# A graph layer on one core: the aggregation's copy and store move to ScalarE, the product weights get a pool of their own, and two products cross a seam between phases

## The chip, the cores and the metric

The kernel runs on one core of a Trainium2 chip. A core has five engines that run side by side, each through its own instructions in order: TensorE (PE, with PEld for its weight loads), VectorE (DVE), ScalarE (ACT), GpSimd (POOL) and SyncE (SP), which here does nothing but issue transfers. ScalarE and GpSimd can issue transfers too. The metric is the device time of one execution in microseconds (us), less is better. Before the change the median of 3 runs is 1910.45 us (1910.1 to 1912.72).

## The reference

One layer over 32 graphs of 512 nodes and 256 features, float32. After a layer norm and a relu, each graph goes through a convolution branch and a message branch, and a gated unit joins them:

```python
h = jnp.maximum(_layernorm(x), 0.0)
# inside the layer, with x for h:
xc = jnp.transpose(x, (0, 2, 1))
c = relu(bn(conv1d(xc, conv1_w, 0)))            # 1 tap
c = bn(conv1d(c, conv2_w, 8))                   # 17 taps
x_conv = jnp.transpose(relu(c + xc), (0, 2, 1))
s = x @ w_se.T + b_se                           # 3 features for each node
A = jnp.exp(-squared_distances(s)) * mask       # mask = adj
msg = relu(x @ w_msg.T + b_msg)
x_nmp = jnp.einsum('bnm,bmd->bnd', A, msg)      # the aggregation
# gi, gh: products of [x_conv, x_nmp] and x with w_ih and w_hh
r, z = sigmoid(gi_r + gh_r), sigmoid(gi_z + gh_z)
n = tanh(gi_n + r * gh_n)
out = x_before_norm + (1 - z) * n + z * x
```

## The kernel before

The 17-tap convolution is done by frequencies: windows of 64 nodes are transformed (`xf`), each frequency unit `u` of 40 is multiplied by the transformed weights (`WD`, in DRAM), and the results (`YD`, in DRAM) are transformed back later. The graphs are cut into two groups of 16. The phases are: first part of group 0 (norm, first convolution, windows to frequencies, and the weights to frequencies), nodes of group 0 (messages, `A`, aggregation, with the 40 products spread between), first part of group 1, nodes of group 1, and then the gated unit for pairs of graphs, from about 911 us to the end. In the first parts the instructions stand in the order in which the program records them; in the nodes phases a scheduler orders them at build time.

The parts that the change and the steps below touch:

```python
    WT, WSUM = {}, {}

    def load_unit(pw, g, u):
        t = WT[g, u] = pw.tile([P, 2, DC, D], FP, tag="wt", name=f"wt_{g}_{u}", bufs=3)
        for k in range(2):
            nc.sync.dma_start(t[:, k], WD[2 * u + k].rearrange("(i p) o -> p i o", p=P))

    def sum_unit(pw, g, u):
        t = WSUM[g, u] = pw.tile([P, DC, D], FP, tag="wsum", name=f"wsum_{g}_{u}", bufs=2)
        nc.gpsimd.tensor_tensor(t, WT[g, u][:, 0], WT[g, u][:, 1], op=ALU.add)

    def product(pw, g, u, xf):
        if (g, u) not in WT:
            load_unit(pw, g, u)
        if u > 0 and (g, u) not in WSUM:
            sum_unit(pw, g, u)
        wt = WT.pop((g, u))
        re, im = xf[:, :, 2 * u, :], xf[:, :, 2 * u + 1, :]
        wr, wi = wt[:, 0], wt[:, 1]
        y = pw.tile([P, 3, D], FP, tag="y", name=f"y_{g}_{u}", bufs=3)
        p = bank(f"py_{g}_{u}")
        if u == 0:
            terms = [(p[:, :D], re, wr), (p[:, D : 2 * D], im, wi)]
        else:
            both = pw.tile([P, 2, DC, P], FP, tag="both", name=f"both_{g}_{u}", bufs=2)
            nc.gpsimd.tensor_tensor(both[:, 0], re, im, op=ALU.add)
            nc.gpsimd.tensor_tensor(both[:, 1], im, re, op=ALU.subtract)
            wsum = WSUM.pop((g, u))
            p2 = bank(f"py2_{g}_{u}")
            terms = [(p2[:, :D], both[:, 1], wr), (p[:, D : 2 * D], both[:, 0], wi), (p[:, :D], re, wsum)]
        for dst, v, w in terms:
            for ic in range(DC):
                nc.tensor.matmul(dst, v[:, ic, :], w[:, ic, :], start=(ic == 0), stop=(ic == DC - 1))
        for k in range(2):
            nc.scalar.copy(by_half(y[:, k, :]), halves(p[:, k * D : (k + 1) * D]))
        if u == 0:
            nc.vector.memset(y[:, 2, :], 0.0)
        else:
            nc.vector.tensor_copy(by_half(y[:, 2, :]), halves(p2[:, :D]))
        nc.scalar.dma_start(YD[g][:, 3 * u : 3 * u + 3, :], y)

```

```python
# VectorE takes mean and variance and normalises, GpSimd takes the power -1/2 (rstd)
    def statistics(b):
        stats = work.tile([P, NC, 6], FP, tag="stats", name=f"stats_{b}")
        mv = work.tile([P, NC, 2], FP, tag="mv", name=f"mv_{b}")
        for c in range(NC):
            nc.vector.bn_stats(stats[:, c, :], X[b][:, c, :])
        for c in range(NC):
            nc.vector.bn_aggr(mv[:, c, :], stats[:, c, :])
        rstd = work.tile([P, NC], FP, tag="rstd", name=f"rstd_{b}")
        STATS[b] = mv, rstd
        nc.vector.tensor_scalar(rstd, mv[:, :, 1], LN_EPS, None, op0=ALU.add)
        nc.gpsimd.tensor_tensor(rstd, rstd, minus_half[:, :NC], op=ALU.pow)

    def normalise(b):
        mv, rstd = STATS.pop(b)
        XN[b] = pools["first"].tile([P, NC, D], FP, tag="xn", name=f"xn_{b}", bufs=2)
        for c in range(NC):
            nc.vector.tensor_scalar(
                by_half(XN[b][:, c, :]), halves(X[b][:, c, :]), mv[:, c, 0:1], rstd[:, c : c + 1],
                op0=ALU.subtract, op1=ALU.mult,
            )
        del X[b]

    def transpose_h(b):
        HT[b] = work.tile([P, DC, N], FP, tag="hT", name=f"hT_{b}")
        for dc in range(DC):
            p = bank(f"phT_{b}_{dc}")
            for c in range(NC):
                nc.tensor.transpose(p[:, c * P : (c + 1) * P], XN[b][:, c, dc * P : (dc + 1) * P], ident)
            nc.vector.tensor_scalar(HT[b][:, dc, :], p, 0.0, None, op0=ALU.max)
        nc.sync.dma_start(HD[b], HT[b])
        del XN[b]

    def by_chunks(b):
        HQ[b] = work.tile([P, DC, N], FP, tag="hq", name=f"hq_{b}", bufs=2)
        for ic in range(DC):
            nc.scalar.copy(chunks(HQ[b][:, ic, :]), by_chunk(HT[b][:, ic, :]))
        del HT[b]
    # (cut) message(b): products hq x wmsg into pm; affinity(b): pd, exponentials e on ScalarE,
    # transposes at<-adj and products A = e * at on VectorE
```

```python
# the aggregation, in the nodes phase

    def aggregate(b):
        NMP[b] = work.tile([P, DC, N], FP, tag="nmp", name=f"nmp_{b}")
        for dc in range(DC):
            p = bank(f"pn_{b}_{dc}")
            for mc in range(NC):
                nc.tensor.matmul(p, MSG[b][:, mc, dc * P : (dc + 1) * P], A[b][:, mc, :],
                                 start=(mc == 0), stop=(mc == NC - 1))
            nc.vector.tensor_copy(NMP[b][:, dc, :], p)
        del MSG[b], A[b]

    def save_nmp(b):
        nc.sync.dma_start(ND[b], NMP.pop(b))
```

```python
    def first_part(g, xf, between):


        b0, b1 = g * GB, (g + 1) * GB
        for b in range(b0, b0 + 3):
            if b not in X:
                load_x(b, nc.gpsimd if g else nc.sync)
        statistics(b0)
        normalise(b0)
        statistics(b0 + 1)
        if g == 0:
            transpose_h(b0)
        normalise(b0 + 1)
        if g > 0:
            transpose_h(b0)
        for b in range(b0, b1):
            if b + 3 < b1:
                load_x(b + 3, nc.gpsimd)
            if b == b0:
                conv1(b)
                if g == 0:
                    for steps in between(0):
                        for step in steps:
                            step()
            if b + 2 < b1:
                statistics(b + 2)
            if b + 1 < b1:
                transpose_h(b + 1)
            if b + 2 < b1:
                normalise(b + 2)
            one, two = between(b - b0) if b > 0 else ([], [])
            if b > b0:
                conv1(b)
            for step in one:
                step()
            if b > b0:
                windows_to_freq(b - 1, xf)
            for step in two:
                step()
        by_chunks(b1 - 1)
        load_h(b0)
        windows_to_freq(b1 - 1, xf)
```

```python
# (cut) the phases; `between` of group 0 spreads the transform of the weights
        # (cut)

            def between(b):
                if b % 2 == 0 and b // 2 + 1 < QI // PI:
                    load_taps(gen, b // 2 + 1)
                if 1 <= b <= len(load_weights):
                    load_weights[b - 1]()
                mine = spread(steps, b, GB - 1) if b < GB - 1 else []
                return mine[:1], mine[1:]

            xf = freq_tile(0)
            with tc.manual_schedule():
                first_part(0, xf, between)


# (cut) in nodes(g, xf, last): units = list(range(UNITS)), UNITS is 40
            for i, b in enumerate(todo):
                mine = spread(units, i, last) if i < last else []
                more = i + 1 < GB
                if more:
                    load_adj(todo[i + 1])
                    factors(todo[i + 1])
                for u in mine[:1]:
                    product(pools["pw"], g, u, xf)
                begin(i + 2)
                if more:
                    affinity(todo[i + 1])
                for u in mine[1:2]:
                    product(pools["pw"], g, u, xf)
                aggregate(b)
                save_nmp(b)
                for u in mine[2:]:
                    product(pools["pw"], g, u, xf)

        with phase("pw"):
            with phase("nodes"):
                nodes(0, xf, GB)
            with phase("first", "sums"):
                combine = combine_weights()

                def between(b):

                    if b == GB - 3:
                        for u in range(3):
                            load_unit(pools["pw"], 1, u)
                    two = [partial(sum_unit, pools["pw"], 1, b - GB + 3)] if b > GB - 3 else []
                    return combine[b - 2] if 1 < b < len(combine) + 2 else [], two

                xf = freq_tile(1)
                with tc.manual_schedule():
                    first_part(1, xf, between)
            with phase("nodes"):
                nodes(1, xf, GB - 3)
    outer.close()
```

A name such as `wt_0` is the weights of unit 0; `py` is a product's bank, `pn` the aggregation's, `pm` the message's, `pd` the distances', `pc` the first convolution's, `px` the windows'. `hq` is a copy of `hT` in another order, made by ScalarE. A matrix product of float32 shows as two records in the trace.

Of the kernel before, what the change touches and what calls it, by code (L numbers as in the profile page):

```python
# [57 lines left out]
def gnn_layer(  # L58
# [33 lines left out]
    outer = ExitStack()  # L92
    work = pools["work"] = outer.enter_context(tc.tile_pool(name="work", bufs=2, reuse_waits="tile"))
    early = outer.enter_context(tc.tile_pool(name="early", bufs=1, reuse_waits="tile"))

    def bank(name):
        return psum.tile([P, N], FP, tag="bank", name=name)
# [223 lines left out]

    WT, WSUM = {}, {}

    def load_unit(pw, g, u):
        t = WT[g, u] = pw.tile([P, 2, DC, D], FP, tag="wt", name=f"wt_{g}_{u}", bufs=3)
        for k in range(2):
            nc.sync.dma_start(t[:, k], WD[2 * u + k].rearrange("(i p) o -> p i o", p=P))

# [3 lines left out]

    def product(pw, g, u, xf):
        if (g, u) not in WT:
            load_unit(pw, g, u)
        if u > 0 and (g, u) not in WSUM:
            sum_unit(pw, g, u)
        wt = WT.pop((g, u))
# [23 lines that stand above are left out]
# [80 lines left out]
# [4 lines that stand above are left out]
            for mc in range(NC):  # L446
                nc.tensor.matmul(p, MSG[b][:, mc, dc * P : (dc + 1) * P], A[b][:, mc, :],  # L447
                                 start=(mc == 0), stop=(mc == NC - 1))
            nc.vector.tensor_copy(NMP[b][:, dc, :], p)
        del MSG[b], A[b]  # L450

    def save_nmp(b):
        nc.sync.dma_start(ND[b], NMP.pop(b))

# [251 lines left out]
        return todo[len(todo) * i // n : len(todo) * (i + 1) // n]  # L708


    def first_part(g, xf, between):


        b0, b1 = g * GB, (g + 1) * GB
# [2 lines left out]
                load_x(b, nc.gpsimd if g else nc.sync)  # L717
        statistics(b0)
        normalise(b0)
        statistics(b0 + 1)  # L720
        if g == 0:
            transpose_h(b0)
        normalise(b0 + 1)
        if g > 0:
            transpose_h(b0)
        for b in range(b0, b1):
            if b + 3 < b1:
                load_x(b + 3, nc.gpsimd)
# [21 lines left out]
        by_chunks(b1 - 1)  # L750
        load_h(b0)
        windows_to_freq(b1 - 1, xf)

    @contextmanager
    def phase(*names, bufs=1):
# [5 lines left out]
    with tc.tile_pool(name="freq", bufs=1) as fpool:  # L761
# [3 lines left out]
        with phase("first", "gen"):  # L765
# [7 lines left out]
            def between(b):  # L773
                if b % 2 == 0 and b // 2 + 1 < QI // PI:
                    load_taps(gen, b // 2 + 1)
                if 1 <= b <= len(load_weights):
                    load_weights[b - 1]()
                mine = spread(steps, b, GB - 1) if b < GB - 1 else []
                return mine[:1], mine[1:]

            xf = freq_tile(0)
            with tc.manual_schedule():
                first_part(0, xf, between)


        def nodes(g, xf, last):


            b1 = (g + 1) * GB
            todo = [b1 - 1] + list(range(g * GB, b1 - 1))  # L790
            units = list(range(UNITS))

            def begin(i):
                if i < GB:
                    if todo[i] not in HQ:
# [28 lines left out]

        with phase("pw"):
            with phase("nodes"):
                nodes(0, xf, GB)
            with phase("first", "sums"):
                combine = combine_weights()

                def between(b):

                    if b == GB - 3:
                        for u in range(3):
                            load_unit(pools["pw"], 1, u)
                    two = [partial(sum_unit, pools["pw"], 1, b - GB + 3)] if b > GB - 3 else []
                    return combine[b - 2] if 1 < b < len(combine) + 2 else [], two

                xf = freq_tile(1)
                with tc.manual_schedule():  # L840
                    first_part(1, xf, between)
            with phase("nodes"):
                nodes(1, xf, GB - 3)
    outer.close()


# [92 lines left out]
```

## Time and profile before

| | before |
|---|---|
| time, median of 3 | 1910.45 us |
| span of the profiled execution | 1907.5 us |
| mean granted TensorE clock | 0.988 |
| VectorE copy `nmp<-pn`, 128x512 (L449) | 64 times, mean 674 ns |
| ScalarE copy `p<-pg`, 128x512 (L583) | 32 times, mean 585 ns |
| GpSimd `wsum<-wt` (L331) | 78 times, mean 1413 ns |
| GpSimd `both<-xf` (L347, L348) | 78 times each, mean 752 and 735 ns |
| DMA `wt<-wd` (SyncE) | 160 of 256 KB, 4.5 us to landing (median) |
| DMA `nd<-nmp` (SyncE) | 32 of 512 KB, 3.2 us to landing (median) |

The profile is one execution. For a group of instructions it gives the busy time, the mean of one, and the idle time of the engine just before them with what ended it, as in `[2.52 <-DVE xn L276]`: the engine was idle for 2.52 us until VectorE's write of `xn` released it. In the timeline the columns are the start (us), the duration (us), the engine, line and operation, what it writes and reads, and how many records are joined in the row. `SPq` and `ACTq` are the issues of transfers on SyncE's and ScalarE's queues. The slices cut the span into 40 equal parts, with the busy share in tenths, and `PEclk` is the TensorE clock that was granted, in tenths.

### The profile page before, as it was taken

The numbers are of one execution on the slowest core, as the hardware profiler recorded it, in microseconds if no ns is written. First come the engines' busy times: TensorE is split into PE (matmuls) and PEld (weight loads), VectorE is DVE, ScalarE is ACT, GpSimd is POOL, SyncE is SP. The second block draws the span as 40 slices with busy tenths as digits, with TensorE's granted clock in tenths as the row PEclk, the third lists the DMA queues.
The fourth block names the chain that finished last, engine by engine and source line by source line (L and its number), as shares of the span: only waits on it lengthen the run. The fifth ranks groups of instructions, "written<-read, shape, count | busy, mean of one in ns | idle before, by whom it ended". The sixth has DMA issues, their size and how long they took to land.

```text
span 1907.5 us, 20922 instructions
## 1 busy us (share of the span) xinstructions
PE 1851.2 (97%) x6976; PEld 1114.8 (58%) x6976; DVE 1127.5 (59%) x2234; ACT 563.8 (30%) x1083; POOL 575.7 (30%) x558
## 2 busy tenths in 40 slices
PE   7998999999799899999999999999999999999997
PEld 5776666666698566666555554555455554555443
DVE  7775556564886455555266456645665456655666
ACT  2455434332245333333222221222122221222121
POOL 3330343333332344444413322133212322133210
PEclk9999999999899999999999999999999999999999
DMA  7999888966467788878622554245522554245512
GB/s 207 295 266 228 248 235 248 270 193 202 156 233 198 212 255 265 257 214 239 191 64 67 130 130 109 48 103 130 128 69 62 130 130 98 64 98 130 130 24 43
DMA packets 336954, 309.89 MB, mean 162 GB/s; under 512 B 148567, under 2 KB 286711, under 8 KB 336463
## 3 DMA queue, kind: packets, MB, share of 16 engines
q1 hardware_dynamic: 314783, 248.87, 49.7%
q0 software_dynamic: 7680, 27.30, 5.3%
q10 hardware_dynamic: 14384, 32.39, 4.8%
q8 instruction: 56, 0.92, 0.2%
q14 instruction: 51, 0.42, 0.1%
HBM read 201.60 MB, written 106.89 MB: 162 GB/s over the span
## 4 chain that ended last, share of the span: by engine, by line
PE 64%; DVE 2%; issue 0%; ACT 0%; DVEq 0%
PE pg L556 29%; PE pn L556 15%; PE pc L545 6%; PE pn L447 5%; PE py L354 5%; PE pm L398 2%; PE pd L433 1%; PE psr L422 0%; DVE rz L887 0%; ACT rz L571 0%; DVE rz L687 0%; DVE rz L664 0%; DVE o L694 0%; DVE nt L688 0%; DVE nt L628 0%
## 5 line engine op out<-in xcount | busy, mean ns | idle before, releaser
L534 POOL TENSOR_TENSOR hp<-hp 128x512 f32<-128x512 f32 x64 | 94.7, 1489 | 466.7 <-DMA hp<-hd 423.9
L556 PE MATMUL pg<-hp,sw 128*128 128x512 f32 x448 | 229.9, 595 | 3.1 <-DVE u L588 3.1
L556 PE MATMUL pg<-np,sw 128*128 128x512 f32 x448 | 229.5, 594 | 0.0
L556 PE MATMUL pg<-cp,sw 128*128 128x512 f32 x448 | 228.8, 592 | 0.0
L447 PE MATMUL pn<-A,msg 128*128 128x512 f32 x512 | 225.0, 593 | 0.0
L447 PEld LDWEIGHTS pn<-A,msg 128*128 128x128 f32 x512 | 97.1, 190 | 110.6 <-issue 108.6
L347 POOL TENSOR_TENSOR both<-xf 128x256 f32<-128x256 f32 x78 | 58.7, 752 | 330.4 <-PE py L354 298.6
L354 PE MATMUL py<-wt,both 128*128 128x256 f32 x624 | 151.9, 387 | 6.3 <-DVE at L438 5.6
L571 ACT ACTIVATE rz<-rz,brz 128x512 f32<-128x512 f32 x96 | 69.3, 722 | 276.9 <-DVE rz L575 276.9
L556 PEld LDWEIGHTS pg<-hp,sw 128*128 128x128 f32 x448 | 85.1, 191 | 110.3 <-issue 101.4
L556 PEld LDWEIGHTS pg<-np,sw 128*128 128x128 f32 x448 | 85.4, 191 | 107.7 <-issue 107.7
L556 PEld LDWEIGHTS pg<-cp,sw 128*128 128x128 f32 x448 | 85.3, 190 | 107.5 <-issue 107.5
L354 PEld LDWEIGHTS py<-wt,both 128*128 128x128 f32 x624 | 115.3, 192 | 50.9 <-issue 35.3
L534 POOL TENSOR_TENSOR cp<-cp 128x512 f32<-128x512 f32 x64 | 80.3, 1266 | 186.4 <-ACT cp L550 185.1
L439 DVE TENSOR_TENSOR A<-e,at 128x512 f32<-128x512 f32 x128 | 114.5, 934 | 30.0 <-ACT e L436 29.9
L300 PE MATMUL pc<-w,hT 128*128 128x256 f32 x512 | 124.2, 399 | 4.7 <-DVE hT L288 4.7
L331 POOL TENSOR_TENSOR wsum<-wt 128x512 f32<-128x512 f32 x78 | 110.1, 1413 | 55.7 <-DMA wt<-wd 55.0
L545 PEld LDWEIGHTS pc<-back,yt 120*128 120x128 f32 x1024 | 116.9, 192 | 7.7 <-issue 7.7
L398 PE MATMUL pm<-wmsg,hq 128*128 128x259 f32 x512 | 117.3, 381 | 0.0
L545 PE MATMUL pc<-back,yt 120*128 120x80 f32 (+1 forms) x1024 | 116.2, 274 | 0.0
L633 ACT ACTIVATE nt<-nt,vech 128x512 f32<-128x512 f32 x64 | 46.2, 722 | 233.9 <-DVE nt L632 233.9
L556 PE MATMUL pn<-hp,sw 128*128 128x512 f32 x224 | 115.1, 595 | 0.0
(123 smaller groups left out, 2854.5 us busy)
## 6 DMA issues: line engine op xcount, KB each, us to landing
wt<-wd SPq DMA_DIRECT2D x160, 256.0 KB, 4.5
adj<-in_adj_dram SPq DMA_DIRECT2D x128, 256.0 KB, 5.5
yd<-y ACTq DMA_DIRECT2D x80, 384.0 KB, 5.2
yt<-yd SPq DMA_DIRECT2D x60, 480.0 KB, 7.9
wd<-wst SPq DMA_DIRECT2D x64, 320.0 KB, 5.0
hd<-hT SPq DMA_DIRECT2D x32, 512.0 KB, 4.3
nd<-nmp SPq DMA_DIRECT2D x32, 512.0 KB, 3.2
xb<-in_x_dram SPq DMA_DIRECT2D x128, 128.0 KB, 3.4
```

The costliest lines, as they stand in the source:

```text
L300: nc.tensor.matmul(p[:, j, :], HT[b][:, ic, c * P : (c + 1) * P], w1[:, ic, :], start=(ic == 0), stop=(ic == DC - 1))
L331: nc.gpsimd.tensor_tensor(t, WT[g, u][:, 0], WT[g, u][:, 1], op=ALU.add)
L347: nc.gpsimd.tensor_tensor(both[:, 0], re, im, op=ALU.add)
L354: nc.tensor.matmul(dst, v[:, ic, :], w[:, ic, :], start=(ic == 0), stop=(ic == DC - 1))
L398: nc.tensor.matmul(p[:, : D + NS], hq[:, ic, c * P : (c + 1) * P], wmsg[:, ic, :], start=(ic == 0), stop=(ic == DC - 1))
L439: nc.vector.tensor_mul(A[b][:, mc, :], e, at)
L447: nc.tensor.matmul(p, MSG[b][:, mc, dc * P : (dc + 1) * P], A[b][:, mc, :], start=(mc == 0), stop=(mc == NC - 1))
L534: nc.gpsimd.tensor_tensor(t[:, dst, :], t[:, a, :], t[:, b, :], op=sub)
L545: nc.tensor.matmul(bk[:, t0:t1], YT[p][j * W + w][:, oc * P : (oc + 1) * P], back[:, u0 : u0 + t1 - t0], start=(w == 0), stop=(w == W - 1) ...
L556: nc.tensor.matmul(bk, sw[:, k, q, o, :], terms[k][q], start=(first and i == 0), stop=(i == len(ks) - 1), skip_group_check=True)
L571: nc.scalar.activation(rz[:, g, j, :], src, AF.Sigmoid, bias=brz[:, g : g + 1], scale=1.0)
L633: nc.scalar.activation(n, n, AF.Tanh, bias=b_in[:, i : i + 1], scale=1.0)
```

## The change

The copy of the aggregation out of its bank goes from VectorE to ScalarE, and its store from SyncE's queue to ScalarE's, so that SyncE's loads no longer stand behind a store that waits for the aggregation. The product weights `wt` get a pool of their own that is open through all phases, so that the first three units of group 0 can be loaded at the end of its first part. The last two products of group 0 are recorded inside the first part of group 1, after the first graph's normalisation, to give TensorE work while that graph is normalised; in the same place the first graph's transpose is now ahead of the second graph's normalisation in both groups.

```diff
--- before.py
+++ after.py
@@ -92,6 +92,7 @@
     outer = ExitStack()
     work = pools["work"] = outer.enter_context(tc.tile_pool(name="work", bufs=2, reuse_waits="tile"))
     early = outer.enter_context(tc.tile_pool(name="early", bufs=1, reuse_waits="tile"))
+    wts = outer.enter_context(tc.tile_pool(name="wts", bufs=3, reuse_waits="tile"))
 
     def bank(name):
         return psum.tile([P, N], FP, tag="bank", name=name)
@@ -321,8 +322,8 @@
 
     WT, WSUM = {}, {}
 
-    def load_unit(pw, g, u):
-        t = WT[g, u] = pw.tile([P, 2, DC, D], FP, tag="wt", name=f"wt_{g}_{u}", bufs=3)
+    def load_unit(g, u):
+        t = WT[g, u] = wts.tile([P, 2, DC, D], FP, tag="wt", name=f"wt_{g}_{u}")
         for k in range(2):
             nc.sync.dma_start(t[:, k], WD[2 * u + k].rearrange("(i p) o -> p i o", p=P))
 
@@ -332,7 +333,7 @@
 
     def product(pw, g, u, xf):
         if (g, u) not in WT:
-            load_unit(pw, g, u)
+            load_unit(g, u)
         if u > 0 and (g, u) not in WSUM:
             sum_unit(pw, g, u)
         wt = WT.pop((g, u))
@@ -446,11 +447,11 @@
             for mc in range(NC):
                 nc.tensor.matmul(p, MSG[b][:, mc, dc * P : (dc + 1) * P], A[b][:, mc, :],
                                  start=(mc == 0), stop=(mc == NC - 1))
-            nc.vector.tensor_copy(NMP[b][:, dc, :], p)
+            nc.scalar.copy(NMP[b][:, dc, :], p)
         del MSG[b], A[b]
 
     def save_nmp(b):
-        nc.sync.dma_start(ND[b], NMP.pop(b))
+        nc.scalar.dma_start(ND[b], NMP.pop(b))
 
 
 
@@ -708,7 +709,7 @@
         return todo[len(todo) * i // n : len(todo) * (i + 1) // n]
 
 
-    def first_part(g, xf, between):
+    def first_part(g, freq, between, left=()):
 
 
         b0, b1 = g * GB, (g + 1) * GB
@@ -717,12 +718,12 @@
                 load_x(b, nc.gpsimd if g else nc.sync)
         statistics(b0)
         normalise(b0)
+        for step in left:
+            step()
+        xf = freq(g)
         statistics(b0 + 1)
-        if g == 0:
-            transpose_h(b0)
+        transpose_h(b0)
         normalise(b0 + 1)
-        if g > 0:
-            transpose_h(b0)
         for b in range(b0, b1):
             if b + 3 < b1:
                 load_x(b + 3, nc.gpsimd)
@@ -750,6 +751,7 @@
         by_chunks(b1 - 1)
         load_h(b0)
         windows_to_freq(b1 - 1, xf)
+        return xf
 
     @contextmanager
     def phase(*names, bufs=1):
@@ -775,21 +777,19 @@
                     load_taps(gen, b // 2 + 1)
                 if 1 <= b <= len(load_weights):
                     load_weights[b - 1]()
-                mine = spread(steps, b, GB - 1) if b < GB - 1 else []
+
+                mine = spread(steps, b, GB - 1) if b < GB - 1 else [partial(load_unit, 0, u) for u in range(3)]
                 return mine[:1], mine[1:]
 
-            xf = freq_tile(0)
             with tc.manual_schedule():
-                first_part(0, xf, between)
-
-
-        def nodes(g, xf, last):
+                xf = first_part(0, freq_tile, between)
+
+
+        def nodes(g, xf, units, last):
 
 
             b1 = (g + 1) * GB
             todo = [b1 - 1] + list(range(g * GB, b1 - 1))
-            units = list(range(UNITS))
-
             def begin(i):
                 if i < GB:
                     if todo[i] not in HQ:
@@ -824,7 +824,7 @@
 
         with phase("pw"):
             with phase("nodes"):
-                nodes(0, xf, GB)
+                nodes(0, xf, range(UNITS - 2), GB)
             with phase("first", "sums"):
                 combine = combine_weights()
 
@@ -832,15 +832,15 @@
 
                     if b == GB - 3:
                         for u in range(3):
-                            load_unit(pools["pw"], 1, u)
+                            load_unit(1, u)
                     two = [partial(sum_unit, pools["pw"], 1, b - GB + 3)] if b > GB - 3 else []
                     return combine[b - 2] if 1 < b < len(combine) + 2 else [], two
 
-                xf = freq_tile(1)
+                left = [partial(product, pools["pw"], 0, u, xf) for u in range(UNITS - 2, UNITS)]
                 with tc.manual_schedule():
-                    first_part(1, xf, between)
+                    xf = first_part(1, freq_tile, between, left)
             with phase("nodes"):
-                nodes(1, xf, GB - 3)
+                nodes(1, xf, range(UNITS), GB - 3)
     outer.close()
 
 

```

## The prediction

> **What bounds the kernel now.** I read first the engines' busy time and the slices of the span, then TensorE's own waits, then the timeline around each wait, and last the waits of SyncE's DMA queue. The busy rows and the slices:
>
> ```profile
> PE 1851.2 (97%) x6976; PEld 1114.8 (58%) x6976; DVE 1127.5 (59%) x2234; ACT 563.8 (30%) x1083; POOL 575.7 (30%) x558
> ...
> PE   7998999999799899999999999999999999999997
> ...
> PEclk9999999999899999999999999999999999999999
> ```
>
> TensorE is busy for 1851.2 of 1907.5 us, so all that a change of schedule can win is the other 56.3 us, plus what its matmuls lose at a lowered clock. The change adds and removes no matmul. The slices have three dips: the start, the slice near 480 us and the end. The change touches neither the first 160 us nor the last part. The list of TensorE's waits (total us, times, longest) names the rest:
>
> ```profile
> PE phT L287 <- DVE xn L276: 11.4, 4, 3.5
> PE py L354 <- DVE at L438: 5.6, 1, 5.6
> PE py L354 <- DMA wt<-wd: 5.4, 1, 5.4
> PE pc L300 <- DVE hT L288: 4.7, 2, 3.6
> ```
>
> Three stretches hold what the change can reach, all at seams between phases; the windows from 200 to 400 us and from 640 to 850 us show TensorE 100% busy.
>
> Seam 1, first part 0 into nodes 0: the first product waits for its weights.
>
> ```profile
> 180.44 2.28 SPq L327 DMA_DIRECT2D wt<-wd  x2
> ...
> 188.81 3.48 PE L354 MATMUL py<-wt,xf 128*128 128x256 f32 x8 [5.43 <-DMA wt<-wd]
> 190.87 1.14 ACT L384 COPY hq<-hT 128x512 f32<-128x512 f32 x2 [5.29 <-DMA hT<-hd]
> ```
>
> The last stores of `wd` are issued from 161.41 to 169.76 us, the next graph's `hT` at 169.85 (landed by 177.09), 2 MB of `adj` from 171.30, and `wt_0` only then. In the 5 us windows from 165 to 200 us the DMA share is 0.89 to 1.25: this seam is a queue of bytes.
>
> Seam 2, nodes 0 into first part 1:
>
> ```profile
> 476.32 0.69 DVE L449 COPY nmp<-pn 128x512 f32<-128x512 f32 x1 [2.74 <-PE pn L447]
> 477.85 1.34 DVE L264 BATCH_NORM_STATS2 stats<-x 128x6 f32<-128x256 f32 x4
> 481.39 2.21 PE L287 MATMUL phT<-ident,xn 128*128 128x128 f32 x8 [2.52 <-DVE xn L276]
> 487.24 6.18 PE L300 MATMUL pc<-w,hT 128*128 128x256 f32 x16 [3.64 <-DVE hT L288]
> 497.72 1.93 PE L287 MATMUL phT<-ident,xn 128*128 128x128 f32 x8 [3.43 <-DVE xn L276]
> ```
>
> VectorE is held at the copy of the last aggregation until 476.32 and only then starts the new group's statistics. Idle time is 2.52 + 3.64 + 3.43 = 9.6 us; and the 16 records of `pc` take 6.18 us here against 3.62 at full clock (granted clock 0.60 in 480 to 490).
>
> Seam 3, early in nodes 1:
>
> ```profile
> 633.45 0.34 SPq L453 DMA_DIRECT2D nd<-nmp  x1
> 634.37 2.16 SPq L327 DMA_DIRECT2D wt<-wd  x2
> 639.48 3.43 PE L354 MATMUL py<-wt,both 128*128 128x256 f32 x8 [5.60 <-DVE at L438]
> ```
>
> The wait is put down to a transpose of `adj`, but what lands just then is the weight load issued at 634.37. That load stood in SyncE's queue behind the store of `nmp`. SyncE's queue had issued `adj` until 619.04 and then nothing for 14 us. The queue's own waits say the same for the whole run:
>
> ```profile
> SPq L453 <- DVE nmp L449: 173.0, 30, 16.9
> ```
>
> [...] 8 `py` records after the 5.43 and 5.60 us gaps take 3.48 and 3.43 us against 1.89 elsewhere, so such a gap costs 1.5 to 1.6 us on top of itself. [...] the trace has 585 (`p<-pg`) and 674 ns (`nmp<-pn`).
>
> **The change part by part.**
>
> *Copies and stores to ScalarE.* 64 copies of 0.674 us (43.0 us) leave VectorE, 64 of about 0.585 us (37.4 us) and 32 issues of 0.34 us go to ScalarE. ScalarE is 30% busy, VectorE 59%. In the steady part TensorE never waits, so this alone is worth nothing there. In the built order ScalarE's two copies come right behind the aggregation and ahead of `sl` and `sr`; these are wanted only after a product (2.6 us) and mostly a message block (3.7 us), so no new wait.
>
> *Seam 3.* With the store gone from SyncE, the order there is `adj`, `wt_3`, `hT_18`. The fourth piece of `adj` and `wt_3` (its buffer is free once the first product has run, 615.8) can go out at about 619.5 and land by about 625; `py_3` is wanted at about 633.9. The gap of 5.60 us and the slow 1.54 us (3.43 - 1.89) go: **-7.1 us**.
>
> *Seam 1.* `wt_0` to `wt_2` are now issued at the end of first part 0, but in SyncE's order they come before `hT_0` and `adj`, and the first of them waits for all outstanding stores of `wd`. In the old order bytes moved at about 0.22 MB/us (2.56 MB `wd` from 161.4, then 0.5 MB `hT`, 2 MB `adj`, 0.5 MB `wt_0`, landed at 188.7: 5.6 MB in about 25 us, with 2 us left for the landing). I estimate the wait for `wd` to end near 172.5, 1.5 MB of weights to be through by about 179, `hT_0` landed at 181 to 184 instead of 177.0. Then the message block of graph 0 starts at about 182.5 instead of 177.90: a gap of about 4 us after the `psr` transposes end at 178.1, with the slow clock behind it (1.5). From 182.5: 3.7 + 1.5 for the block, 1.1 `pd`, 0.9 transposes, 1.9 for `py_0` without a wait, 191.6. The old order had `py_0` done at 192.1 and the next block at 192.13, held by `hT_1` (190.87 + its copy). `hT_1` now comes behind 1 MB more of weights and the bubble, 192 to 194. So the gap moves from weights to `hT` and the later point shifts by 0 to +2: **+1 us**, uncertain by 3 either way.
>
> *Seam 2.* Two products (2.6 us each) move behind the last aggregation, and the statistics no longer stand behind its copy. Were that all, the 7.8 us of three products would cover 1.91 (statistics) + 1.04 (`rstd` on GpSimd) + 1.38 (normalise). But the built order on GpSimd is: x loads, `rstd` of graph 16, then `wsum_38`, `both_38`, `wsum_39`, `both_39`. So product 38 waits for `rstd`, which waits for the statistics, which stand on VectorE behind the copy for product 37, which follows the last aggregation. Counting from the end of the last aggregation: that copy starts at 1.06 and ends 1.48; statistics until 3.4; `rstd` 4.45; `wsum_38` 1.27, 5.7; `both_38` 0.72 + 0.73, 7.2. Product 37 ends at 2.6. So TensorE is idle for about 4.7 us before product 38, which then runs 1.5 slower: 11.4; product 39 to 14.0; then `phT` to 15.0 without a wait. The order of transpose and normalise is turned, so `hT` is evicted at once: the `hT` wait shrinks from 3.64 to about 1, `pc_16` ends near 20. The next wait, `phT` of graph 18 (statistics 1.9, `rstd` 1.1, normalise behind the `hT` evictions), stays at about 3.4: `pc_17` starts at about 26. Old order on the same work: the last aggregation would have ended at 476.12 - 5.2 = 470.9, `pc_17` started at 499.44, 28.5. **-2.5 us**.
>
> Sum: -7.1 + 1 - 2.5 = -8.6; 1910.45 - 8.6 = 1901.9, rounded to 1902.
>
> **The rivals.** (a) Seam 2 is hidden as meant, because `rstd` is done before product 38 wants its operands. For it: GpSimd is only 30% busy. Against it: the order in the built program, in which the statistics can't start before product 37. It would take another 6.2 us off (4.7 + 1.5), 1896. (b) Seam 1 gets worse: the wait for `wd` drains the queue, and `hT_0`, `adj` and `hT_1` all come later by the full 1.5 MB. For it: DMA shares near or over 1 there; against it: part of the weights' bytes only trade places. 1.5 MB at 0.22 MB/us is 6.8 us, 6 more than I took: 1908. (c) ScalarE, in order, holds up the exponentials or the sigmoid inputs of the next graph behind its wait for the aggregation, and TensorE waits once in each graph. For it: at the first graph of nodes 1 two exponentials now stand between the two copies. Against it: they are wanted a whole graph later. At 0.5 us in 32 graphs it would more than cancel the gain: 1918. (d) Seam 3 goes on waiting, since `adj` is the true releaser: no gain there, 1909.
>
> **Range and chances.** Seam 3 is the surest (worth 7.1 with a fault of 1.5), seams 1 and 2 by 3 each; root of the squares about 4.5, so 1902 with 1896 to 1909 for 8 in 10. 2% is 38 us: to gain that, two thirds of all idle time in the run would have to go; to lose it, something in every graph would have to wait over 1 us. So 0.02 faster, 0.97 within, 0.01 slower.
>
> **What would show it.** In the changed profile: no wait of `py` for weights of 5 us in nodes 1; a wait of `pm` for `hT` (ScalarE `hq`) near 178 to 182 in place of the 5.43; a wait of `py` for GpSimd `both` or `wsum` of about 5 us near 475; the wait of `pc` for `hT` under 1.5 us; 100% busy windows between 200 and 400 us as before. Wrong if `phT` follows the products with no idle before product 38, if the steady windows fall under 99%, or if the first seam's lost time differs from the old one by over 4 us.

## The result and the profile after

The changed kernel takes 1907.73 us (median of 4 runs, 1904.07 to 1909.81) against 1910.28 (4 runs, 1908.69 to 1912.72) beside it: a ratio of 0.9983 with an interval of 0.9964 to 1.0003. Run once more with later experiments it took 1905.74 us (22 runs) against 1909.84 (43 runs), 0.9979 (0.997 to 0.9988). The first interval includes no gain at all, the second does not. So the change gains 2.6 to 4.1 us. The prediction had 8.45 (1902 against 1910.45).

The busy rows and the slices on the page of the changed kernel (its profiled execution took 1904.07 us, the lowest of the first four):

```profile
PE 1848.2 (97%) x6976; PEld 1112.1 (58%) x6976; DVE 1097.1 (58%) x2170; ACT 598.5 (31%) x1147; POOL 578.7 (30%) x558
...
PE   7998999999899999999999999999999999999997
```

The 64 copies and 32 issues have moved: VectorE has 64 instructions fewer, ScalarE 64 more. The slice from 618 us on, where seam 3 lies, is full now; the one near 480 us is still short, and so is the one from 143 to 190 us, in which seam 1 begins (it was so before). TensorE's waits in the changed kernel (us in total, times, longest):

```profile
PE pm L399 <- ACT hq L385: 9.8, 2, 6.4
PE phT L288 <- DVE xn L277: 8.8, 3, 3.5
...
PE py L355 <- POOL both L349: 4.5, 1, 4.5
...
PE pc L301 <- DVE hT L289: 1.5, 2, 1.1
```

Both waits of `py` for weights are gone. In their place the message block waits twice for `hq` (9.8 us in all), and one product waits for GpSimd.

**Seam 1**, SyncE's queue and TensorE in the kernel before, beside the lines that the prediction shows:

```profile
169.85 1.08 SPq L372 DMA_DIRECT2D hT<-hd  x1
171.30 9.04 SPq L368 DMA_DIRECT2D adj<-in_adj_dram  x8
172.64 3.67 PE L398 MATMUL pm<-wmsg,hq 128*128 128x259 f32 x16
182.84 0.42 SPq L372 DMA_DIRECT2D hT<-hd  x1
199.49 7.03 PE L447 MATMUL pn<-A,msg 128*128 128x512 f32 x16
```

and SyncE's queue, ScalarE and TensorE in the changed kernel:

```profile
160.65 8.32 SPq L250 DMA_DIRECT2D wd<-wst  x8
171.89 3.66 PE L399 MATMUL pm<-wmsg,hq 128*128 128x259 f32 x16
172.75 2.94 SPq L328 DMA_DIRECT2D wt<-wd  x6
175.74 0.47 SPq L373 DMA_DIRECT2D hT<-hd  x1
176.31 10.25 SPq L369 DMA_DIRECT2D adj<-in_adj_dram  x8
...
182.99 1.14 ACT L385 COPY hq<-hT 128x512 f32<-128x512 f32 x2 [5.01 <-DMA hT<-hd]
183.66 5.31 PE L399 MATMUL pm<-wmsg,hq 128*128 128x259 f32 x16 [6.35 <-ACT hq L385]
186.66 1.24 SPq L373 DMA_DIRECT2D hT<-hd  x1
...
195.22 1.14 ACT L385 COPY hq<-hT 128x512 f32<-128x512 f32 x2 [0.58 <-DMA hT<-hd]
195.89 5.53 PE L399 MATMUL pm<-wmsg,hq 128*128 128x259 f32 x16 [3.42 <-ACT hq L385]
...
205.11 7.03 PE L448 MATMUL pn<-A,msg 128*128 128x512 f32 x16
```

SyncE issues nothing for 3.8 us after the last store of `wd` (168.97 to 172.75; the DMA share from 170 to 175 us falls to 0.46, before it was 0.89), then the six weight loads, and only then `hT_0`. The first gap of 6.35 us is followed by a message block at 5.31 us instead of 3.67, the second of 3.42 us by one at 5.53. Gaps and slow blocks lose 6.35 + 1.64 + 3.42 + 1.86 = 13.3 us; before, the 5.43 us wait and the slow product (3.48 - 1.89) lost 7.0. From the first message block of the phase to its first aggregation it took 26.85 us before and takes 33.22 now: **+6.4**.

**Seam 2**, TensorE's timeline in the changed kernel:

```profile
483.78 3.66 PE L355 MATMUL py<-wt,both 128*128 128x256 f32 x8 [4.46 <-POOL both L349]
...
492.21 3.89 PE L301 MATMUL pc<-w,hT 128*128 128x256 f32 x16 [0.45 <-DVE hT L289]
...
500.41 2.27 PE L288 MATMUL phT<-ident,xn 128*128 128x128 f32 x8 [3.43 <-DVE xn L277]
```

The transposes `phT` of the first graph follow the products without a wait, but product 38 waits 4.46 us for GpSimd and then runs slow (3.66 us instead of 1.89, with a granted clock of 0.50 from 484 to 486 us). The `hT` wait is down from 3.64 to 0.45, the last `phT` wait is what it was. **-2.6 us** on the same work, from the fourth message block of nodes 0 to the second convolution block.

**Seam 3**, SyncE's queue and TensorE in the changed kernel:

```profile
605.40 17.14 SPq L369 DMA_DIRECT2D adj<-in_adj_dram  x12
622.65 6.75 SPq L328 DMA_DIRECT2D wt<-wd  x2
...
635.59 1.89 PE L355 MATMUL py<-wt,both 128*128 128x256 f32 x8
```

In the kernel before, the queue's last row ahead of its hole was

```profile
603.51 15.53 SPq L368 DMA_DIRECT2D adj<-in_adj_dram  x11
```

The hole of 14 us (619.04 to 633.45) is filled: the weights go out from 622.65 instead of 634.37, and the product starts without a wait. **-7.3 us** from the first message block of nodes 1 to the fourth. The windows between the seams (220 to 460 and 645 to 900 us) are full as before (TensorE busy for 240.0 of 240 us and 253.9 of 255, before 240.0 and 254.3).

### The profile page after: what moved, and what is told of

Its sections match the earlier page's. It is cut to its first block, busy times and chain, and to the rows that moved or that the text cites. A ratio compares the mean times of both kernels' runs of the same rounds, so it can differ in the third digit from the quotient of the medians.

```text
span 1902.3 us, 20941 instructions
## 1 busy us (share of the span) xinstructions
PE 1848.2 (97%) x6976; PEld 1112.1 (58%) x6976; DVE 1097.1 (58%) x2170; ACT 598.5 (31%) x1147; POOL 578.7 (30%) x558
## 4 chain that ended last, share of the span: by engine, by line
PE 90%; DVE 3%; DMA 3%; SPq 1%; issue 1%; POOL 1%; ACT 0%; POOLq 0%; DVEq 0%; ACTq 0%
PE pg L557 29%; PE pn L557 15%; PE pn L448 11%; PE py L355 11%; PE pc L546 6%; PE pm L399 6%; PE pc L301 4%; PE px L316 3%; PE pw L237 2%; PE pd L434 2%; PE phT L288 1%; DMA ws<-w 1%; PE psr L423 1%; DMA wt<-wd 1%; DVE stats L265 1%
## 5 line engine op out<-in xcount | busy, mean ns | idle before, releaser
L440 DVE TENSOR_TENSOR A<-e,at 128x512 f32<-128x512 f32 x128 | 114.8, 936 | 37.0 <-ACT e L437 36.9
L361 DVE COPY y<-py 128x256 f32<-128x256 f32 x78 | 32.8, 420 | 158.1 <-PE py L355 157.3
L301 PE MATMUL pc<-w,hT 128*128 128x256 f32 x512 | 119.8, 388 | 1.5 <-DVE hT L289 1.5
```

What stands on the lines that cost most here:

```text
L301: nc.tensor.matmul(p[:, j, :], HT[b][:, ic, c * P : (c + 1) * P], w1[:, ic, :], start=(ic == 0), stop=(ic == DC - 1))
L440: nc.vector.tensor_mul(A[b][:, mc, :], e, at)
```

## The experiments

All times are medians, and all ratios are to the kernel before, run beside each batch (1910.28 us in the first, then 1910.63, 1909.84 and 1909.82). For comparison each trace is read in three stages. A goes from the first message block of nodes 0 to the fourth, B from there to the second convolution block of the first part of group 1, and C from the first message block of nodes 1 to the fourth. Each stage holds the same work in all kernels, so that the left-over products need no correction. A, B and C are one trace each.

| kernel | us | ratio (interval) | A | B | C |
|---|---|---|---|---|---|
| before | 1910.28 | | 36.85 | 289.95 | 40.28 |
| changed | 1907.73 | 0.9983 (0.9964 to 1.0003) | 43.23 | 287.35 | 32.97 |
| changed, again | 1905.74 | 0.9979 (0.997 to 0.9988) | 44.65 | 287.99 | 32.97 |
| no early weights | 1899.98 | 0.995 (0.9937 to 0.9963) | 35.20 | 288.10 | 33.00 |
| store on SyncE | 1911.04 | 1.0008 (0.9997 to 1.002) | 41.37 | 288.23 | 40.11 |
| sums first | 1903.65 | 0.9966 (0.9954 to 0.9977) | 41.63 | 284.90 | 32.96 |
| no products left over | 1903.49 | 0.9966 (0.9956 to 0.9976) | 44.16 | 287.16 | 32.97 |
| `hT` first | 1900.74 | 0.9952 (0.9937 to 0.9966) | 36.06 | 288.13 | 32.97 |
| one unit early | 1903.75 | 0.9964 (0.9951 to 0.9978) | 37.42 | 287.09 | 32.96 |
| before + order | 1908.26 | 0.9991 (0.9984 to 0.9998) | 36.11 | 287.38 | 40.15 |
| copy on VectorE | 1903.38 | 0.9963 (0.9949 to 0.9976) | 44.01 | 287.38 | 33.01 |
| before + store | 1901.8 | 0.9954 (0.9941 to 0.9967) | 36.83 | 289.97 | 33.00 |
| two mends | 1895.68 | 0.9925 (0.9912 to 0.9937) | 36.33 | 283.39 | 32.99 |
| two mends, early statistics | 1892.61 | 0.9906 (0.989 to 0.9922) | 34.50 | 281.96 | 32.97 |

Outside these stages one execution differs from the next: the first message block of nodes 0 starts between 170.0 and 176.5 us in these traces, in the changed kernel itself at 171.89 and at 176.54, and the stretch between B and C takes 101.8 to 106.3 us, in the changed kernel itself 102.75 and 106.25. In A kernels with the same loads differ by up to 3.3 us, in B kernels with the same seam by up to 1.1, in C by 0.2. So a stage shows more than the total does, a difference in A from two single traces is uncertain by some 3 us, and differences of totals under 2 us are not read here.

### Leaving out the early weight loads

```diff
-  mine = spread(steps, b, GB - 1) if b < GB - 1 else [partial(load_unit, 0, u) for u in range(3)]
+  mine = spread(steps, b, GB - 1) if b < GB - 1 else []
```

> The changed kernel without the loads of wt_0 to wt_2 at the end of first part 0 (they are left to the nodes phase; in the built order hT_0 stands first again, then wt_0, hT_1, adj). Theory: the first seam lost its time because 1.5 MB of weights go ahead of hT_0 and hT_1 in SyncE's order. From the start of the first message block to the start of the first aggregation the kernel before takes 26.9 us and the changed one 33.2; here it should be 27 or less, and the whole about 6 us less than the changed kernel, 1901 to 1902. Rival: the seam is a queue of bytes and the order does not matter; then 33 us stays and the time stays near 1907. A second rival, that ScalarE's new copies hold up the first seam, also leaves 33 us.

1899.98 us, 5.8 under the changed kernel's 1905.74 of another batch; stage A is down from 43.23 to 35.20. SyncE's queue and TensorE in this kernel:

```profile
166.92 1.19 SPq L373 DMA_DIRECT2D hT<-hd  x1
171.13 0.89 SPq L328 DMA_DIRECT2D wt<-wd  x2
172.12 0.42 SPq L373 DMA_DIRECT2D hT<-hd  x1
172.59 10.32 SPq L369 DMA_DIRECT2D adj<-in_adj_dram  x8
...
175.29 3.67 PE L399 MATMUL pm<-wmsg,hq 128*128 128x259 f32 x16
181.69 1.34 PE L434 MATMUL pd<-sr,sl 9*128 9x512 f32 x8 [2.73 <-ACT sr L425]
184.08 2.81 PE L355 MATMUL py<-wt,xf 128*128 128x256 f32 x8
186.72 3.67 PE L399 MATMUL pm<-wmsg,hq 128*128 128x259 f32 x16
```

Both message blocks run without a wait and at full clock (3.67 us each), and `py_0` does not wait for its weights either, though they were not loaded early. What is left there is a wait of 2.73 us for ScalarE's `sr`, which stands in ScalarE's order behind `hq` of the next graph (179.33), and behind it a lowered clock (0.50 from 183 to 185 us; `py_0` 2.81 instead of 1.89). The early loads cost 8.0 us in this stage by these two traces, and 7.2 by the means of all traces with the three units (43.2, six traces) and without any (36.0, six). ScalarE's copies and the weights' own pool are in this kernel too, so neither is the cause. The loads move bytes that nobody wants yet ahead of bytes that hold up TensorE.

The order here is not that of the kernel before either: there `wt_0` and `hT_1` go out behind eight pieces of `adj` (180.44 and 182.84), here ahead of them (171.13 and 172.12). Stage A is 36.1 to 36.9 us with the old order and 34.5 to 36.3 with this one, three traces each, which do not tell the two apart.

### Putting the store back on SyncE

```diff
-        nc.scalar.dma_start(ND[b], NMP.pop(b))
+        nc.sync.dma_start(ND[b], NMP.pop(b))
```

> The changed kernel with the store of nmp back on SyncE's queue; the copy stays on ScalarE. Theory: in nodes 1 the weights of unit 3 again stand behind the store, TensorE waits 5 to 6 us for them and runs slow for 1.5 us: from the first message block of group 1 to that of its third graph 40 us as before (40.3), not 33.0; whole time about 7 us over the changed kernel, 1914 to 1915. Rival: what mattered was the copy on ScalarE or the own pool of the weights, and the store's queue is nothing: 33 us and 1907.

1911.04 us: stage C is back at 40.11. TensorE's timeline in this kernel:

```profile
639.92 3.63 PE L355 MATMUL py<-wt,both 128*128 128x256 f32 x8 [5.22 <-DMA wt<-wd]
```

The same gap with the same slow product behind it as before (there 5.60 and 3.43 us), and this time the profile names the weights as the releaser. Seam 3 is the place of the store in SyncE's order and nothing else. Without this part, what is left of the change gains nothing that these runs resolve.

### The sums of the left products ahead of the statistics

A function takes the `wsum` and `both` of products 38 and 39 out of `product`, and the first part of group 1 begins with it:

```diff
+        for step in ahead:      # wsum and both of units 38 and 39
+            step()
         statistics(b0)
         normalise(b0)
```

> The changed kernel with GpSimd's sums for products 38 and 39 recorded ahead of the statistics of the first graph, so that they stand before rstd in its order. Theory: the 4.5 us wait of product 38 and its slow matmuls go, and nothing else takes their place, since rstd then ends about 6.4 us after the last aggregation and the transposes are wanted at 7.8: from the end of the last aggregation to the second conv block of group 1 about 20 us instead of 25.9; whole time 6 us less, 1901 to 1902. Rival: the later rstd only moves the wait to the transposes (25 us stays).

1903.65 us; stage B goes from 287.35 to 284.90. TensorE's timeline in this kernel:

```profile
481.13 1.99 PE L364 MATMUL py<-wt,both 128*128 128x256 f32 x8 [1.06 <-POOL both L345]
...
486.69 5.57 PE L301 MATMUL pc<-w,hT 128*128 128x256 f32 x16 [1.82 <-DVE hT L289]
```

The 4.46 us wait shrinks to 1.06, and its slow clock goes (product 38 takes 1.99 us instead of 3.66). That would be 5.1 us (3.4 and 1.7). But only 2.5 come out, because the wait of `pc` for `hT` grows from 0.45 to 1.82 and `pc` now runs at a lowered clock (0.50 from 488 to 490 us). The order on GpSimd was the cause of product 38's wait, and its removal uncovers the next wait on VectorE.

### No products left over

```diff
-                nodes(0, xf, range(UNITS - 2), GB)
+                nodes(0, xf, range(UNITS), GB)
-                left = [partial(product, pools["pw"], 0, u, xf) for u in range(UNITS - 2, UNITS)]
+                left = [partial(product, pools["pw"], 0, u, xf) for u in ()]
```

> The changed kernel with all 40 products of group 0 in its nodes phase, none in the next first part. Theory: the two moved products are worth little, because their sums wait for rstd; without them the statistics come behind the copy of product 39, the transposes wait 2 to 3 us and the hT eviction still comes early, so the second seam costs about what it costs in the changed kernel: whole time within 2 us of it (1905 to 1910). Rival: the moved products are what gained 2.6 us at this seam; without them it falls back to 28.5 us, 1910, or more, because the statistics now wait with nothing beside them (5 us, 1913).

Stage B is 287.16 with all 40 products in the nodes phase, and 287.35 in the changed kernel. TensorE's timeline of this kernel at the seam:

```profile
487.67 2.21 PE L288 MATMUL phT<-ident,xn 128*128 128x128 f32 x8 [2.53 <-DVE xn L277]
490.94 5.60 PE L301 MATMUL pc<-w,hT 128*128 128x256 f32 x16 [1.06 <-DVE hT L289]
```

The wait of `phT` that the two products were to fill is back (2.53), and the wait for GpSimd is gone: the stage is as long. The gain of seam 2 was already there without the products. The time of 1903.49 us (14 runs) lies 7.1 under the kernel before, though the three stages account for 2.8 of it only. In its trace another 2.1 us lie between B and C and 1.0 ahead of A, both of which differ by as much between two executions of one kernel, and its A (44.16) is at the upper end of what these loads gave. Against the changed kernel (1905.74) its interval overlaps. Whether leaving the two products over costs something elsewhere stays open.

### The changed kernel again

> The changed kernel itself, once more beside the kernels of this batch. If the four experiments before it are read rightly, it lies about 7 us above the kernel without the early weight loads (1900.0) and about 7 us under the kernel with the store on SyncE (1911.0): 1904 to 1907. The times of the one run so far go from 1904 to 1910.

1905.74 us over 22 runs, from 1900.32 to 1914.57. Its profiled execution was the slowest of them, 1914.57 us, and is useful for that: compared with the first trace, the start is 4.65 us longer, stage A 1.4, stage B 0.6, C equal, and the stretch between B and C 3.5 (106.25 against 102.75). The profile of one execution can thus lie several us away from the median.

### The order of two lines alone, in the kernel before

```diff
-        if g == 0:
-            transpose_h(b0)
+        transpose_h(b0)
         normalise(b0 + 1)
-        if g > 0:
-            transpose_h(b0)
```

> The kernel before with one line's move alone: the first graph's transpose ahead of the second graph's normalisation in both groups; no products left over, copy on VectorE, store on SyncE, no early weights. Theory: all of seam 2's gain comes from this order: the wait of pc for hT goes from 3.64 to about 1.1, the first part of group 1 starts its second convolution block 2.6 to 2.8 us sooner, time 1908. Rival (the gain comes from the products that fill the gap, or from the copy's leaving VectorE): the time given back at the wait of phT, 1910.6 as before.

1908.26 us, and stage B 287.38 against 289.95: **-2.6**, the whole gain of seam 2. TensorE's timeline:

```profile
478.38 1.89 PE L287 MATMUL phT<-ident,xn 128*128 128x128 f32 x8 [2.52 <-DVE xn L276]
481.65 6.09 PE L300 MATMUL pc<-w,hT 128*128 128x256 f32 x16 [1.37 <-DVE hT L288]
```

The first wait is as before and the second falls from 3.64 to 1.37: VectorE evicts `hT` before it normalises the next graph. The total falls by 1.6 us; its interval (0.4 to 3.1 us) holds the 2.6.

### The store alone, in the kernel before

```diff
-        nc.sync.dma_start(ND[b], NMP.pop(b))
+        nc.scalar.dma_start(ND[b], NMP.pop(b))
```

> The kernel before with one line's move alone: the aggregation's store on ScalarE's queue, the copy still on VectorE. Theory: seam 3 goes from 40.2 to 33.0 us, the other two stay at 36.9 and 23.3; time 7.2 under the kernel before, 1903. Rival (ScalarE, in order, is held by a store that waits for VectorE's copy, so the copy has to move too): the gain shrinks by what TensorE then waits in each graph, 1905 to 1912.

1901.8 us, 8.0 under the kernel before: this line alone is worth more than the whole change. SyncE's queue and TensorE in nodes 1:

```profile
603.45 16.09 SPq L368 DMA_DIRECT2D adj<-in_adj_dram  x12
619.65 7.62 SPq L327 DMA_DIRECT2D wt<-wd  x2
...
633.64 1.89 PE L354 MATMUL py<-wt,both 128*128 128x256 f32 x8
```

Stage C is 33.00, A and B are those of the kernel before. A store that waits for VectorE's copy on ScalarE's queue costs nothing that shows: the windows 220 to 460 and 645 to 900 us have TensorE busy for 240.0 and 254.3 us, as in the kernel before.

### The copy back on VectorE

```diff
-            nc.scalar.copy(NMP[b][:, dc, :], p)
+            nc.vector.tensor_copy(NMP[b][:, dc, :], p)
```

> The changed kernel with the aggregation's copy back on VectorE; its store stays on ScalarE. Theory (who copies is off the path, since TensorE is busy without a gap in the steady stretch): seam 1 43 us, seam 2 26, seam 3 33, time as the changed kernel, 1905.7. Rival (VectorE's 43 us more hold up the products A, or ScalarE's store now waits for VectorE): 1907 to 1912.

1903.38 us; A, B and C are those of the changed kernel within their spread. ScalarE's copies take a mean of 586 ns in the changed kernel and VectorE's 674 ns here, and neither stands on the path. The total is 2.4 us under that of the changed kernel in another batch, and the intervals of the two ratios overlap (0.9949 to 0.9976 and 0.997 to 0.9988). As with the left products, the stages don't show where, so that a small cost of ScalarE's copy can't be excluded.

### One unit early

```diff
-  ... else [partial(load_unit, 0, u) for u in range(3)]
+  ... else [partial(load_unit, 0, u) for u in range(1)]
```

> Only the first unit's weights are loaded early, ahead of hT_0: 0.5 MB instead of 1.5. Theory of the drain (hT_0 is late because the weight load ahead of it waits until wd's last stores have landed, 3.8 us, in which SyncE issues nothing): two thirds of the bytes go, but the wait stays; hT_0 is issued only some 2 us earlier, the seam takes 30 to 32 us against 33.2, time about 2 us under the changed kernel. Theory of bytes: 1 MB less at 0.22 MB/us lets hT_0 and hT_1 land about 4.5 us earlier each; the seam takes 27 to 29, time 5 to 6 us under it.

Stage A is 37.42, 27.42 to the first aggregation, which is what the theory of bytes had. SyncE's queue and TensorE in this kernel:

```profile
176.19 0.90 SPq L328 DMA_DIRECT2D wt<-wd  x2
177.13 0.47 SPq L373 DMA_DIRECT2D hT<-hd  x1
...
183.35 5.51 PE L399 MATMUL pm<-wmsg,hq 128*128 128x259 f32 x16 [2.66 <-ACT hq L385]
195.14 3.85 PE L399 MATMUL pm<-wmsg,hq 128*128 128x259 f32 x16 [2.78 <-ACT hq L385]
```

The 4.0 us in which SyncE waits for `wd` (172.16 to 176.19) are still there, as the theory of the drain had it. Counted from the first message block (175.27), the block of graph 0 starts at 8.08 us, in the changed kernel (171.89) at 11.77: the other 1 MB had delayed it by 3.7 us, of which 2.0 are the issue of four more loads on SyncE (0.49 us each) and the rest the way of `hT_0` from its issue to the start of its copy `hq` (7.2 us there; 5.6 here by an estimate that takes `hq` to start as long ahead of the block as there). Of the 8.0 us that the early loads cost, some 5.8 hang on the two units that no product wanted before 200 us, and the other 2.2 are left with the first unit: the wait for `wd`, and `hT_1` behind `adj`. These are single traces in a stage uncertain by some 3 us, so that the larger part is shown and the smaller is not. The total (6.1 us under the kernel before, 2.0 under the changed one) shows less than the stage; it is what the theory of the drain had.

### `hT` first, then the weights

```diff
         load_h(b0)
+        if g == 0:
+            load_h(b0 + 1)
+            load_unit(0, 0)
+            load_unit(0, 1)
         windows_to_freq(b1 - 1, xf)
```

(and no weight loads in the place where the changed kernel has them)

> The early loads are kept but stand behind both hT_0 and hT_1 and ahead of adj; only two units. Theory of order (what hurts is that hT stands behind weights that wait for wd): no wait of pm for hq over 1 us, from the start of the first message block to the first aggregation 25 us or less against 33.2, time 1900 or under. Theory of bytes (the first aggregation comes when the same 5.6 MB are through, in whatever order): the wait moves to adj or to a product, 27 us or more there, about 1903.

1900.74 us. No message block waits; the first aggregation comes 19.62 us after the first message block, the earliest of all. But then, on TensorE:

```profile
199.34 1.10 PE L355 MATMUL py<-wt,both 128*128 128x256 f32 x4 [1.38 <-DMA wt<-wd]
203.56 1.76 PE L355 MATMUL py<-wt,both 128*128 128x256 f32 x4 [3.12 <-DMA wt<-wd]
```

The third unit, now behind twelve pieces of `adj`, comes late, and stage A takes 36.06 us, no better than without early loads. Both theories hold a part: the order decides whether `hT` waits, and the bytes come back one product later.

### Both mends, and the last wait

The changed kernel without early loads and with the sums first:

> The changed kernel without the early weight loads, and with the sums of the two left products ahead of the new group's statistics. Theory (the two seams are independent): seam 1 takes 35.2 us from the first message block of the nodes phase to the fourth, as without the early loads alone, seam 2 23.5 as with the early sums alone, time 1897. Rival (one takes back what the other gives): about 1900, as without the early loads alone.

1895.68 us: A 36.33, B 283.39. Both gains are there together, A as without the early loads and B as with the sums first. On top of that, the third graph's statistics and normalisation go ahead of the first graph's convolution in group 1 (their old place behind it, taken out, is not shown):

```diff
         transpose_h(b0)
         normalise(b0 + 1)
+        if g > 0:
+            statistics(b0 + 2)
+            normalise(b0 + 2)
```

> As the one before, and in the first part of group 1 the third graph's statistics and normalisation also come ahead of the first graph's convolution instead of behind it. Theory (the last wait of seam 2, phT for xn, 3.4 us and the slow clock behind it, is there because VectorE does the third graph's statistics after the evictions of the first convolution): the wait goes, seam 2 takes 18 to 20 us, time 1893. Rival (VectorE, GpSimd then hold up the second graph's hT): at most 1 us gained, 1896 to 1897.

1892.61 us, 0.9906 (0.989 to 0.9922): the fastest of all, 17 us under the kernel before. TensorE's timeline:

```profile
480.55 5.57 PE L301 MATMUL pc<-w,hT 128*128 128x256 f32 x16 [1.83 <-DVE hT L289]
485.96 1.91 PE L288 MATMUL phT<-ident,xn 128*128 128x128 f32 x16
488.84 3.89 PE L301 MATMUL pc<-w,hT 128*128 128x256 f32 x16 [0.96 <-DVE hT L289]
```

The 3.43 us wait of `phT` is gone, and 0.96 us for `hT` comes in its place. From the last aggregation to the second convolution block it takes 20.3 us, a little more than the theory had. Stage B falls by 1.4 and not by 3 as the total does; in these two traces another 1.8 lie in A, where the two kernels are the same. `pc` ran at a lowered clock here (5.57 us, 0.50 from 482 to 484 us) and at full clock (3.89 us, 1.00 from 483 to 487) in the trace without the early statistics.

## Why the prediction missed

**Seam 3, -7.1: right.** The prediction's reading of the slices named three dips; the line that it shows has two more, from 143 to 191 and from 620 to 668 us, the places of seams 1 and 3, which its list of waits then found. Measured -7.3. The store alone gives it (stage C 33.00) and its return takes it (40.11). The reading that weights and not `adj` end that wait, against the releaser that the profile named, was right; rival (d) is out.

**Seam 2, -2.5: right in the sum and in its parts.** Measured -2.6 (seven traces with this seam lie between -1.7 and -2.9), with a wait of 4.46 us before product 38 (predicted 4.7), the slow clock behind it (3.66 us instead of 1.89), and the last `phT` wait left at 3.43. What the prediction did not say is that the gain belongs to the order of two lines: alone in the kernel before it gives the same 2.6. The two left products bring nothing in this stage, because they trade a wait of 2.52 us for VectorE for one of 4.46 for GpSimd. Rival (a) put 6.2 us on the removal of that wait; tried, it gave 2.5.

**Seam 1, +1: this step failed, and with it the sum.** The prediction had seen the mechanism: `hT_0` landed at 181 to 184 (measured: by 182.99), a gap (about 4 us in the working, 6.35 measured) and then the slow clock (a block of 5.31 us instead of 3.67). The term that was mis-sized is "the later point shifts by 0 to +2", the start of the block that `hT_1` holds. Counted from the first message block it was 19.49 us before and is 24.00 now, +4.5, and the block itself runs slow, another 1.86: +6.4 in all. The term rested on `hT_1` at 192 to 194; it came at 195.22, which is 5.1 us later than before, counted from the last store of `wd` (21.1 and 26.2 us). The thought behind it was that part of the weights' bytes "only trade places". That holds for `wt_0` against `hT_1`, which it stood ahead of before too. It does not hold for `wt_1` and `wt_2`, which are wanted only behind `py_0` and stood behind `hT_1`; and `hT_0` now waits for all three. At the prediction's own 0.22 MB/us the 1 MB of `wt_1` and `wt_2` is 4.5 us (an estimate), 195.4 instead of 192 to 194. Of the second gap (3.42 us) the working had at most 2.5 us (191.6 to 194.1), of the slow block behind it nothing.

With +6.4 in place of +1 the sum is -7.3 - 2.6 + 6.4 = -3.5, between the two measured differences, -2.6 and -4.1. That is rival (b), which had put the extra at 6 us and the time at 1908. The evidence for it had been laid out (a DMA share near or over 1 in these windows), and the choice against it was the error. Six traces with the three early units have stage A at 41.4 to 44.7 us, and six without any of them (the kernel before, the two additions to it, and three of the mends) at 34.5 to 36.9.

**ScalarE as a new bound, rival (c): out.** The steady windows lost 0.4 us in all, where the rival had 0.5 in each of 32 graphs.

What moving the store brings is not the time of its start: that took 0.34 us on SyncE (633.45, kernel before) and 0.33 on ScalarE (changed kernel), while moving it to the other engine gained 7.3 us in stage C (40.28 to 33.00), because loads had stood behind it in SyncE's order while it waited. In seam 1 the larger part came with the loads of two units (5.8 of 8.0 us in single traces), and there the one other order that was tried did not beat leaving the early loads out.

## What to carry to other kernels

Before loading something earlier, ask when it is first wanted and what will then stand behind it in the same queue: at the seam here, with a DMA share of 0.94 to 1.25 from 175 to 200 us, it was paid by the loads that the next block waited for. Put a store that waits for a late result on a queue in which no load stands behind it; here that one line, alone, did more than the whole change (8.0 us against 2.6 to 4.1). When several parts are changed together, run each alone, since a good part (-7.3) and a bad one (+6.4) can look like a small gain.

## What was not expected of the hardware

The clock also fell after shorter gaps than those of 5.43 and 5.60 us at which the prediction read it. In the kernel before, the gap of 2.52 us ahead of `phT` alone was followed by a granted clock of 0.50 (483 to 485 us; `phT` 2.21 instead of 1.04). With the sums first, gaps of 1.06 and 1.82 us with 3.7 us of work between them were followed by 0.50; in the kernel with two mends, gaps of 0.58 and 1.82 us with the same work between them were not. The windows of the first and of the second (the columns are the window, its length, the busy time and records of PE, PEld, DVE, ACT and POOL, PEclk, DMA share and GB/s):

```profile
488.00:490.00 2.00, 2.00 (x7) 1.55 (x6) 0.86 (x3) 0.00 (x0) 0.00 (x0) 0.50 0.91 266
```

```profile
485.00:487.00 2.00, 2.00 (x11) 1.77 (x10) 1.05 (x3) 0.63 (x1) 0.00 (x0) 1.00 1.02 274
```

The same 16 records of `pc` took 5.57 and 3.89 us. Nor does the length of the gap decide in these traces: in the kernel with one unit early, a gap of 2.78 us behind 9 us of work was followed by a message block of 3.85 us, where the one behind the gap of 2.66 us took 5.51. What decides is not settled by these runs.
